# A macaron transformer on one core: the turned query by two transfers between partitions instead of a second product

## The chip, the cores and the metric

One core of a Trainium2 chip runs the whole program in one launch. The metric is the time of one execution on the device, in microseconds (us). The kernel before was timed in three runs: 1578.59, 1580.87 and 1582.71 us, so its median is 1580.87 us. The profile is of one further execution, which took 1578.82 us.

## What is computed

The input is x of 16 rows, each 512 tokens by 128 features, in float32. Six sublayers follow each other, each with a layer norm in front and a residual sum behind:

1. a small piecewise network per token ("kan" in the code), with half weight
2. causal attention with 16 query heads and 4 key and value heads of 8 features each, and a rotary embedding on queries and keys
3. the network of 1 again, with half weight
4. a mixture of 8 experts; each expert takes the 128 best tokens of each row; with half weight
5. a linear recurrence over the tokens, in pairs of rows
6. the mixture of 4 again, with half weight

The change lies in sublayer 2, in the rotary embedding of the queries. The reference writes it as

```python
def rotate_half(x):
    half = x.shape[-1] // 2
    x1, x2 = (x[..., :half], x[..., half:])
    return jnp.concatenate((-x2, x1), axis=-1)
...
q = (x @ Wq).reshape(bsz, seq_len, NH, HD).transpose(0, 2, 1, 3)
...
q = q * cos + rotate_half(q) * sin
k = k * cos + rotate_half(k) * sin
```

So of the 8 features of a head, the first four take the last four with a minus sign, and the last four take the first four, each times the sine of the token's angle.

## The kernel before

**Layout.** Inside the attention a row's queries lie with 128 partitions = 16 heads x 8 features (head by head) and the 512 tokens along the free axis. `attn_in` (L435) makes them. It normalises the row (`norm`, L296, with a turned copy of it through TensorE in `turned`, L333), multiplies it by `wq` into the PSUM tile `ps_pa` (L443), and VectorE multiplies that by the cosine table `rope[:, 0, :]` into `rope_a` (L444). The rotated query is a second product, of the same row by `wqr`, which is `wq` with the halves of each head exchanged (L572, L573), into `ps_pb` (L449). VectorE multiplies it by the sine table `rope[:, 1, :]`, which holds the sign, into `rope_b` (L450), and GpSimd adds the two (L465). Keys and values come from `ps_kv` (L457, L461).

**Splitting and packs.** The scores are made with bfloat16 products that together keep float32 accuracy: `parts` (L406) splits the sum into three bfloat16 parts, one step on ScalarE (L409) and three on GpSimd (L412, L415, L418), into `qpart`. `spread` (L421) stores the three parts to a scratch tensor `qs` in device memory (L425), `spread_keys` (L428) those of the keys to `ks`. From there the packs `qp` (four a row, in ten buffers) and `kp` (one a row, in three) are loaded (L508, L514), each as soon as its buffer's readers have been issued (the counter `taken`). All of these transfers are on SyncE's queue.

**Steps and turns.** The attention runs in steps, b = -1 to 15. In step b, `weights` (L699) makes the transposed scores of row b (L712), their exponentials on ScalarE (L715), and the causal mask on GpSimd (L717); `maxima` (L638) makes the scores of row b+1 (L652) and their row maxima on VectorE (L657, and L662 where several heads share a bank). `outputs` (L723) multiplies by the values (L738). Scores take their PSUM banks in turn from five (`next_bank`, L630), two a turn. A step has 44 turns: four packs by the eleven banks of `BANKS` (L624).

**Order within the engines.** The order on TensorE, VectorE, ScalarE and GpSimd is the order in which the Python program issues (`manual_schedule`, L222); SyncE's queue is ordered by the scheduler. All other work is written as generators: `stage_in` (kan of a row, then `attn_in`), `stage_out` (L770: the attention's output product through the tile `yT`, the second kan, then `gated`, L793, the normalisation (L320) and gate scores (L799) for the experts). Each generator goes on by one `yield` a turn. In the steady part (`paced`) each turn has a budget for every engine:

```python
MOST = {"pe": 1.5, "dve": 1.15, "act": 0.85, "pool": 1.45}
```

`need(...)` waits for a turn whose budget has that much left and takes it, `take(...)` takes without waiting, `bank(..., work)` waits for one of two PSUM tiles and for TensorE's budget. A reader of a PSUM tile is put in `later`, and issued at the begin of the next turn. Generators that stand earlier in the list are served first. `rope_b` and `yT` have the same tag and so share one buffer. At the end of a step `finish` runs turns of side work alone until the row after next is in.

The ramp is what comes before step 0 (`filling`): rows 0, 1 and 2 go through `attn_in` there; rows 3 to 15 go through it in steps 0 to 12. After step 15 come the experts and the recurrence.

Of the kernel before, what the change touches and what calls it, by code (L numbers as in the profile page):

```python
# [8 lines left out]
F32 = mybir.dt.float32  # L9
# [5 lines left out]
ALU = mybir.AluOpType  # L15
# [33 lines left out]
def tile_macaron(  # L49
# [55 lines left out]
    with ExitStack() as ph:  # L105
# [69 lines left out]
        kcst = cst.tile([P, D], F32, name="kcst")  # L175


        wq = cst.tile([D, NH, HD], F32, name="wq")
        nc.sync.dma_start(out=wq, in_=wq_in.rearrange("k (h d) -> k h d", d=HD))
        wk = cst.tile([D, 2, HD, NR], F32, name="wk")  # L180
        nc.sync.dma_start(out=wk[:, 0, :, :].rearrange("k d h -> k (d h)"), in_=wk_in)
        wv = cst.tile([D, KR], F32, name="wv")
        nc.sync.dma_start(out=wv, in_=wv_in)
        wo = cst.tile([D, D], F32, name="wo")
        rope = cst.tile([P, 2, S], F32, name="rope")
        nc.sync.dma_start(out=rope, in_=rope_in)
        out_weights()
        for b in range(1, B):
            load(b)
# [5 lines left out]
        wqr = cst.tile([D, NH, HD], F32, name="wqr")  # L195
# [41 lines left out]
        def need(**work):  # L237
            while paced[0] and any(w > room[e] for e, w in work.items()):
                yield
            for e, w in work.items():  # L240
                room[e] -= w

        def take(**work):

            for e, w in work.items():
                room[e] -= w
# [7 lines left out]
            for _ in range(turns if hurry[0] else 0):  # L254
                yield

        held, kan_held, hurry = [0], [0], [False]
# [75 lines left out]
        def turned(src, name, pool):  # L333
            ps = yield from bank([P, NT, P], F32, "ps_t", 0.55)
            for c in range(NT):
                nc.tensor.transpose(ps[:, c, :], src[:, c, :], ident)  # L336
            dst = pool.tile([P, S], F32, name=name)
            later.append(lambda: nc.scalar.copy(dst, ps.rearrange("p c q -> p (c q)")))
            yield
            take(act=0.6)  # L340
            freed()
            yield
            yield from rest(1)
            yield
            return dst
# [75 lines left out]
        def spread(part, heads, name):  # L421

            scr = tc.dram_tile([3, HD, heads, S], BF16, name=name)
            for i in range(3):
                nc.sync.dma_start(out=scr[i].rearrange("d h t -> h d t"), in_=part[:, i, :])  # L425
            return scr

        def spread_keys(part, name):  # L428
# [6 lines left out]
        def attn_in(b, st):  # L435
            _, xT = yield from norm(x[b])
            ka = w1p.tile([P, 2, P], F32, name="rope_ka")
            ta = w1p.tile([P, S], F32, name="rope_a")
            tb = w1p.tile([P, S], F32, name="rope_b", tag="yT")
# [3 lines left out]
            nc.tensor.matmul(pa, lhsT=wq.rearrange("k h d -> k (h d)"), rhs=xT, start=True, stop=True)  # L443
            later.append(lambda: nc.vector.tensor_mul(ta, pa, rope[:, 0, :]))  # L444
            yield
            take(dve=0.7)
            freed()
            pb = yield from bank([P, S], F32, "ps_pb", 0.9)
            nc.tensor.matmul(pb, lhsT=wqr.rearrange("k h d -> k (h d)"), rhs=xT, start=True, stop=True)  # L449
            later.append(lambda: nc.vector.tensor_mul(tb, pb, rope[:, 1, :]))  # L450
            yield
            take(dve=0.7)
            freed()
            pkv = yield from bank([P, 3, P], F32, "ps_kv", 1.3)
            for w in range(2):
                for j in range(NT):
                    nc.tensor.matmul(pkv[j * KR : (j + 1) * KR, w, :], lhsT=wk[:, w, :, :].rearrange("k d h -> k (d h)"),  # L457
                                     rhs=xT[:, bass.ts(j, P)], start=True, stop=True)
            pv = pkv[:, 2, :].rearrange("p (c n) -> p c n", n=KR)
            for c in range(NT):  # L460
                nc.tensor.matmul(pv[:, c, :], lhsT=xT[:, bass.ts(c, P)], rhs=wv, start=True, stop=True)  # L461
            later.append(lambda: nc.vector.tensor_mul(ka, pkv[:, 0:2, :], ropek))
            yield
            yield from need(pool=1.25)
            nc.gpsimd.tensor_tensor(ta, ta, tb, ALU.add)  # L465
            take(dve=0.4)

            va = VA[b % len(VA)]
            mine = [va[:, :, j::2, 2 * HD * j : 2 * HD * (j + 1)] for j in range(2)]
            if b < len(VA):  # L470
                nc.gpsimd.memset(va, 0.0)
                for to in mine:
                    nc.gpsimd.memset(to[:, :, :, HD : HD + 1], 1.0)

            def values():
                from_ = pv.rearrange("p c (r j d) -> p c r j d", j=2, d=HD)
                for j, to in enumerate(mine):
                    nc.vector.tensor_copy(to[:, :, :, 0:HD], from_[:, :, :, j, :])

            later.append(values)  # L480
            yield
            take(dve=0.4)
            freed()
            st["va"] = va
            if paced[0]:
# [18 lines left out]
            N = 3 * HD  # L504
            while taken[0] < NR * (b - NKP + 1):
# [35 lines left out]
        def prepare():  # L541
# [22 lines left out]
            freed()  # L564
            yield
            psc = yield from bank([P, 3, P], F32, "ps_kc3")
            centered(psc[:, 0, :], wq.rearrange("k h d -> k (h d)"))
# [4 lines left out]
            nc.vector.tensor_copy(wqr[:, :, 0:hh], wq[:, :, hh:HD])  # L572
            nc.vector.tensor_copy(wqr[:, :, hh:HD], wq[:, :, 0:hh])  # L573
# [196 lines left out]
        def stage_out(b, st):  # L770
            while len(st["out"]) < NR:
                yield
            if paced[0]:
                yield
                yield
            yT = yield from turned(st["y"].rearrange("p c r g d -> p c (r g d)"), "yT", w1p)
# [534 lines left out]
```

## Time and profile before

| what | value |
|---|---|
| median of three runs | 1580.87 us (1578.59 to 1582.71) |
| the profiled execution | 1578.82 us |
| its span, first to last instruction | 1577.0 us |
| mean granted TensorE clock | 0.985 |
| transfers on SyncE's and ScalarE's queues (q1) | 15.0% of 16 engines' span |
| L443 and L449, 32 records each (16 rows, two passes) | 0.593 us and 0.592 us a record |
| L444 and L450, 16 each | 0.678 us each |
| L465, 16 | 1.272 us each |
| L425, issue on SyncE's queue, 48 | 0.570 us each |

The profile names engines PE (TensorE matmul), PEld (its weight loads), DVE (VectorE), ACT (ScalarE), POOL (GpSimd) and SP (SyncE); a trailing q is an engine's queue. It gives for each engine the busy time, the share of the span, and the number of instructions; then the span in 40 equal slices, one digit each for the busy tenths, with 9 for 90% or more (a slice is 39.4 us). The chain of waits is the work that ended last, followed back from the last instruction to whatever released it; its rows have the start, the duration, the engine, the tile written and the line. The table of stretches gives for a part of the span its length, then the busy time and count of PE, PEld, DVE, ACT and POOL, then the granted clock, the share of the transfer engines, and GB/s. One product of the program in float32 appears as two records, of which the second begins before the first has ended.

### The profile page before, as it was taken

The page shows a single profiled execution, that of the slowest core. Times are in us where ns is not written, and L with a number is a line of the kernel's source. Part 1 is how long each engine was busy: PE and PEld are TensorE (multiplying, and loading weights), DVE is VectorE, ACT ScalarE, POOL GpSimd, SP SyncE. Part 2 cuts the span into 40 slices and gives each one's busy share as a digit, 9 for nine tenths or more (in the row PEclk, how much of TensorE's full clock was granted, in tenths as well). Part 3 has the DMA queues.
Part 4 walks back from the last instruction along what each step waited for, and adds up shares of the span by engine and source line. Part 5 has one row for each costly group of instructions (what it writes and reads, how often), then busy time and mean ns, then how long its engine had stood idle before and what let it go on. Part 6 is the DMA issues. An engine that isn't in the chain of part 4 may idle for free.

```text
span 1577.0 us, 33209 instructions
## 1 busy us (share of the span) xinstructions
PE 1480.0 (94%) x11889; PEld 1044.6 (66%) x11905; DVE 1085.1 (69%) x3574; ACT 960.5 (61%) x1852; POOL 923.8 (59%) x1439
## 2 busy tenths in 40 slices
PE   5679999999999999999999899999999999999997
PEld 2334454445445454444444489999998999999997
DVE  5587877878788788888888245865579665753333
ACT  3455767778788777777776865444454444544443
POOL 2535545556655564556454766667666666767773
PEclk8889999999999999999999999999999999999999
DMA  5220110122111210221031113222332233333332
GB/s 136 78 62 29 58 53 14 49 59 60 32 37 54 60 52 14 56 61 41 26 91 53 52 45 71 58 61 70 73 72 61 71 73 62 81 65 68 68 68 61
DMA packets 107467, 92.89 MB, mean 59 GB/s; under 512 B 23469, under 2 KB 95862, under 8 KB 107062
## 3 DMA queue, kind: packets, MB, share of 16 engines
q1 hardware_dynamic: 84464, 67.67, 15.0%
q0 software_dynamic: 21584, 22.89, 7.8%
q8 instruction: 94, 1.54, 0.4%
q14 instruction: 71, 0.58, 0.1%
q10 hardware_dynamic: 1254, 0.20, 0.1%
HBM read 59.20 MB, written 35.45 MB: 60 GB/s over the span
## 4 chain that ended last, share of the span: by engine, by line
PE 78%; DVE 11%; ACT 4%; issue 2%; POOL 1%; DMA 1%; SPq 1%; ACTq 0%; DVEq 0%; POOLq 0%
PE ps_h L1025 14%; PE ps_y L1038 14%; PE ps_av L738 9%; PE ps_st L712 7%; PE ps_sc L652 6%; PE acc L989 5%; DVE below L657 4%; PE ps_kg L385 4%; PE ps_s L356 3%; PE ps_t L336 3%; ACT pt L715 2%; PE ps_x L954 2%; PE ps_g L799 2%; ACT kan_h L375 1%; PE ps_ko L399 1%
## 5 line engine op out<-in xcount | busy, mean ns | idle before, releaser
L715 ACT ACTIVATE pt<-ps_st 128x512 f32<-128x512 f32 (+1 forms) x704 | 378.9, 567 | 127.2 <-PE ps_st L712 115.4
L717 POOL TENSOR_SCALAR_AFFINE_SELECT pt<-pt 128x128 f32<-128x128 f32 (+2 forms) x704 | 252.5, 367 | 315.2 <-ACT pt L715 309.1
L657 DVE CUSTOM_DVE_ANT_0 below<-ps_sc,causal 128x512 bf16<-128x512 f32 (+1 forms) x512 | 315.5, 616 | 102.1 <-PE ps_sc L652 86.2
L934 POOL DMA_INDIRECT xg<-xnd,tokI x256 | 253.0, 988 | 80.8 <-issue 36.4
L1027 ACT ACTIVATE mo<-ps_h 128x512 f32<-128x512 f32 x256 | 152.8, 597 | 217.3 <-PE ps_h L1025 215.2
L1025 PE MATMUL ps_h<-xin,mw 128*128 128x128 f32 x2048 | 272.5, 276 | 0.0
L1038 PE MATMUL ps_y<-mw,mo 128*128 128x128 f32 x2048 | 270.8, 275 | 0.0
L712 PE MATMUL ps_st<-qp,kp 128*128 128x512 bf16 (+3 forms) x1008 | 247.3, 301 | 24.7 <-DVE topped L657 18.6
L652 PE MATMUL ps_sc<-kp,qp 96*128 96x512 bf16 (+3 forms) x1024 | 255.0, 303 | 10.5 <-ACT pt L715 6.6
L1025 PEld LDWEIGHTS ps_h<-xin,mw 128*128 128x128 f32 x2048 | 250.3, 192 | 12.4 <-issue 9.9
L1038 PEld LDWEIGHTS ps_y<-mw,mo 128*128 128x128 f32 x2048 | 249.4, 192 | 1.0 <-DVE ye L1035 0.8
L712 PEld LDWEIGHTS <-kp 128*128 128x128 bf16 x1024 | 94.9, 100 | 191.3 <-issue 171.5
L375 ACT ACTIVATE kan_h<-kan_s,rbias,kw 128x512 f32<-128x512 f32 x256 | 207.5, 820 | 0.0
L1055 POOL DMA_INDIRECT sum<-mo,tokI x93 | 151.5, 1629 | 72.2 <-issue 15.9
L738 PE MATMUL ps_av<-pt,va 128*32 128x512 f32 (+3 forms) x2048 | 165.4, 440 | 1.4 <-POOL pt L717 1.2
L662 DVE TENSOR_REDUCE topped<-ps_sc 128x2 f32<-128x512 f32 (+1 forms) x192 | 127.0, 682 | 23.2 <-PE ps_sc L652 22.6
L652 PEld LDWEIGHTS <-qp 96*128 96x128 bf16 x1024 | 95.5, 98 | 67.2 <-issue 40.7
L738 PEld LDWEIGHTS ps_av<-pt,va 128*32 128x32 f32 x2048 | 53.4, 109 | 87.7 <-issue 44.2
L310 POOL TENSOR_TENSOR ln_rstd<-ln_rstd,mhalf 128x4 f32<-128x4 f32 x96 | 102.3, 1066 | 8.0
L309 POOL TENSOR_SCALAR ln_rstd<-ln_mv 128x4 f32<-128x4 f32 x96 | 22.1, 230 | 135.4 <-DVE ln_mv L307 134.5
L1044 DVE SCALAR_TENSOR_TENSOR ye<-ps_y,gainT,ye 128x128 fp32r<-128x128 f32 x83 | 29.0, 349 | 84.2 <-ACT ye L1041 84.0
L1044 DVE SCALAR_TENSOR_TENSOR parts<-ps_y,gainT,parts 128x128 fp32r<-128x128 f32 x80 | 27.9, 349 | 83.9 <-ACT parts L1041 83.8
(202 smaller groups left out, 2279.4 us busy)
## 6 DMA issues: line engine op xcount, KB each, us to landing
qp<-qs SPq DMA_DIRECT2D x64, 288.0 KB
xnd<-kan_x SPq DMA_DIRECT2D x32, 256.0 KB
sum<-x SPq DMA_DIRECT2D x62, 128.0 KB
qs<-qpart SPq DMA_DIRECT2D x48, 128.0 KB
kp<-ks SPq DMA_DIRECT2D x48, 96.0 KB
x<-in_L_attn_x_dram SPq DMA_DIRECT2D x16, 256.0 KB
mw<-in_L_ffn_w_dram SPq DMA_DIRECT2D x16, 256.0 KB
xg<-xnd,tokI POOLq DMA_INDIRECT x256, 2.5
```

Source lines behind the costliest of these rows:

```text
L375: nc.scalar.activation(h, sk[half], AF.Relu, bias=rbias[:, half, v : v + 1], scale=kw1[:, half, v : v + 1])
L652: nc.tensor.matmul(v[:, u, 0:n], lhsT=qp[r][0:MXR, g, bass.ts(c, P)], rhs=kp[0:MXR, r, 0:n], start=alone, stop=(u == len(gs) - 1), skip_gr ...
L657: nc.vector.tensor_tensor_reduce(below[:, 0:n], v[:, 0, 0:n], causal[:, S - n : S], 1.0, LOWEST, ALU.add, ALU.max, accum_out=maxs[:, h, c ...
L712: nc.tensor.matmul(v[:, u, 0:n], lhsT=kp[ROWS, r, bass.ts(c, P)], rhs=qp[r][ROWS, g, c * P : S], start=True, stop=True)
L715: nc.scalar.activation(o, v[:, :, 0:n], AF.Exp, scale=HD ** -0.5)
L717: nc.gpsimd.affine_select(out=dg, in_=dg, compare_op=ALU.is_ge, fill=0.0, base=0, pattern=[[0, len(gs)], [1, P]], channel_multiplier=-1)
L738: nc.tensor.matmul(po[32 * g : 32 * g + 32, c * P : S], lhsT=va[:, c, r, :], rhs=pt[:, g, OFF[c] : OFF[c] + n], start=(c == 0 and not odd) ...
L934: nc.gpsimd.indirect_dma_start(out=xgs[i // E % 2][:, i % E, :], out_offset=None, in_=xnd[b], in_offset=bass.IndirectOffsetOnAxis(ap=tokI[ ...
L1025: nc.tensor.matmul(pst[:, f, :], lhsT=mw1[e][:, bass.ts(f, P)], rhs=xins[i // E % 2][:, i % E, :], start=True, stop=True)
L1027: nc.scalar.activation(hs[u], pst, AF.Gelu)
L1038: nc.tensor.matmul(py, lhsT=hs[u][:, f, :], rhs=mw2[e][:, f, :], start=(f == 0), stop=(f == NF - 1))
L1055: nc.gpsimd.indirect_dma_start(out=sums[k, b], out_offset=bass.IndirectOffsetOnAxis(ap=tokI[g][:, n : n + 1], axis=0), in_=added[b % 2 * ( ...
```

## The change

For the rows of the ramp (`direct`) little is different: the rotated query is still a second product, and as the sine table is stored differently, GpSimd subtracts instead of adding. For all later rows the second product is gone. VectorE multiplies `ps_pa` twice, first by the sine table into a float32 view of `qpart`, then by the cosine table into `rope_a`. Two transfers of 64 partitions by 512 float32 values carry the first result to the other half of the partitions, into `rope_b`, and GpSimd adds four turns later than it did. For this the partitions are ordered feature by feature (`(d h)` instead of `(h d)`), so that the two halves of all heads lie in the two halves of the partitions; `wq`, `wqr`, the table and the stores to `qs` follow that order, and the table is loaded in four transfers. A flag, `y_held`, keeps `rope_b` and `yT` from holding their buffer at once. In the steady part, three turns lie between the stores to `qs` and `ks` and the loads of the packs.

```diff
-        wq = cst.tile([D, NH, HD], F32, name="wq")
-        nc.sync.dma_start(out=wq, in_=wq_in.rearrange("k (h d) -> k h d", d=HD))
+        wq = cst.tile([D, HD, NH], F32, name="wq")
+        nc.sync.dma_start(out=wq.rearrange("k d h -> k (d h)"), in_=wq_in)
...
-        nc.sync.dma_start(out=rope, in_=rope_in)
+        halves = [slice(a * P // 2, (a + 1) * P // 2) for a in range(2)]
+        for a in range(2):
+            for w in range(2):
+                rows = a ^ w
+                src = rope_in[rows * HD // 2 : (rows + 1) * HD // 2, w, :]
+                nc.sync.dma_start(out=rope[halves[a], w, :], in_=src.unsqueeze(1).to_broadcast([HD // 2, NH, S]))
...
-                nc.sync.dma_start(out=scr[i].rearrange("d h t -> h d t"), in_=part[:, i, :])
+                nc.sync.dma_start(out=scr[i].rearrange("d h t -> (d h) t"), in_=part[:, i, :])
...
-            later.append(lambda: nc.vector.tensor_mul(ta, pa, rope[:, 0, :]))
-            yield
-            take(dve=0.7)
-            freed()
-            pb = yield from bank([P, S], F32, "ps_pb", 0.9)
-            nc.tensor.matmul(pb, lhsT=wqr.rearrange("k h d -> k (h d)"), rhs=xT, start=True, stop=True)
-            later.append(lambda: nc.vector.tensor_mul(tb, pb, rope[:, 1, :]))
-            yield
-            take(dve=0.7)
-            freed()
+            direct = filling[0]
+            if direct:
...
+            else:
+                while y_held[0]:
+                    yield
+                y_held[0] = True
+                unturned = qpart.rearrange("p i t -> p (i t)")[:, 0 : 2 * S].bitcast(F32)
+                later.append(lambda: nc.vector.tensor_mul(unturned, pa, rope[:, 1, :]))
+                yield
+                take(dve=0.7)
+                yield from need(dve=0.7)
+                nc.vector.tensor_mul(ta, pa, rope[:, 0, :])
+                freed()
+                tb = w1p.tile([P, S], F32, name="rope_b", tag="yT")
+                for a in range(2):
+                    nc.sync.dma_start(out=tb[halves[a], :], in_=unturned[halves[1 - a], :])
...
-            yield from need(pool=1.25)
-            nc.gpsimd.tensor_tensor(ta, ta, tb, ALU.add)
+            if direct:
+                yield from need(pool=1.25)
+                nc.gpsimd.tensor_tensor(ta, ta, tb, ALU.subtract)
+                y_held[0] = False
             take(dve=0.4)
...
             st["va"] = va
+            if not direct:
+                for _ in range(4):
+                    yield
+                yield from need(pool=1.25)
+                nc.gpsimd.tensor_tensor(ta, ta, tb, ALU.add)
+                y_held[0] = False
+                yield
             if paced[0]:
                 yield
             qp_steps = parts(ta, qpart, nc.scalar.copy, 1.15, act=0.6)
...
             qs = spread(qpart, NH, f"qs{b}")
             N = 3 * HD
+            for _ in range(3 if paced[0] else 0):
+                yield
             while taken[0] < NR * (b - NKP + 1):
                 yield
...
+            while y_held[0]:
+                yield
+            y_held[0] = True
             yT = yield from turned(st["y"].rearrange("p c r g d -> p c (r g d)"), "yT", w1p)
             po = yield from bank([P, NT, D], F32, "ps_o", 0.9)
             for c in range(NT):
                 nc.tensor.matmul(po[:, c, :], lhsT=yT[:, bass.ts(c, P)], rhs=wo, start=True, stop=True)
+            y_held[0] = False
```

More of the change, by code (lines that the diff above doesn't have):

```diff
@@ L194, in tile_macaron @@
         hh = HD // 2
-        wqr = cst.tile([D, NH, HD], F32, name="wqr")
+        wqr = cst.tile([D, HD, NH], F32, name="wqr")
         identb = cst.tile([P, P], BF16, name="identb")
@@ L255, in rest @@
                 yield
-        held, kan_held, hurry = [0], [0], [False]
+        held, kan_held, hurry, y_held = [0], [0], [False], [False]
         def bank(shape, dtype, name, work=0.0):
@@ L438, in attn_in @@
             ta = w1p.tile([P, S], F32, name="rope_a")
-            tb = w1p.tile([P, S], F32, name="rope_b", tag="yT")
             qpart = w1p.tile([P, 3, S], BF16, name="qpart")
@@ L442, in attn_in @@
             pa = yield from bank([P, S], F32, "ps_pa", 0.9)
-            nc.tensor.matmul(pa, lhsT=wq.rearrange("k h d -> k (h d)"), rhs=xT, start=True, stop=True)
-            later.append(lambda: nc.vector.tensor_mul(ta, pa, rope[:, 0, :]))
-            yield
-            take(dve=0.7)
-            freed()
-            pb = yield from bank([P, S], F32, "ps_pb", 0.9)
-            nc.tensor.matmul(pb, lhsT=wqr.rearrange("k h d -> k (h d)"), rhs=xT, start=True, stop=True)
-            later.append(lambda: nc.vector.tensor_mul(tb, pb, rope[:, 1, :]))
-            yield
-            take(dve=0.7)
-            freed()
+            nc.tensor.matmul(pa, lhsT=wq.rearrange("k d h -> k (d h)"), rhs=xT, start=True, stop=True)
+            direct = filling[0]
+            if direct:
+                later.append(lambda: nc.vector.tensor_mul(ta, pa, rope[:, 0, :]))
+                yield
[4 more added lines that the diff above has]
+                y_held[0] = True
+                pb = yield from bank([P, S], F32, "ps_pb", 0.9)
+                nc.tensor.matmul(pb, lhsT=wqr.rearrange("k d h -> k (d h)"), rhs=xT, start=True, stop=True)
+                tb = w1p.tile([P, S], F32, name="rope_b", tag="yT")
+                later.append(lambda: nc.vector.tensor_mul(tb, pb, rope[:, 1, :]))
+                yield
+                take(dve=0.7)
+                freed()
+            else:
[5 more added lines that the diff above has]
+                yield
+                take(dve=0.7)
+                yield from need(dve=0.7)
+                nc.vector.tensor_mul(ta, pa, rope[:, 0, :])
+                freed()
+                tb = w1p.tile([P, S], F32, name="rope_b", tag="yT")
+                for a in range(2):
+                    nc.sync.dma_start(out=tb[halves[a], :], in_=unturned[halves[1 - a], :])
             pkv = yield from bank([P, 3, P], F32, "ps_kv", 1.3)
@@ L484, in attn_in @@
             st["va"] = va
+            if not direct:
[4 more added lines that the diff above has]
+                y_held[0] = False
+                yield
             if paced[0]:
@@ L504, in attn_in @@
             N = 3 * HD
+            for _ in range(3 if paced[0] else 0):
+                yield
             while taken[0] < NR * (b - NKP + 1):
@@ L566, in prepare @@
             psc = yield from bank([P, 3, P], F32, "ps_kc3")
-            centered(psc[:, 0, :], wq.rearrange("k h d -> k (h d)"))
+            centered(psc[:, 0, :], wq.rearrange("k d h -> k (d h)"), wq)
             centered(psc[:, 1, :], wk[:, 0, :, :].rearrange("k d h -> k (d h)"), wk[:, 0, :, :])
@@ L571, in prepare @@
             yield
-            nc.vector.tensor_copy(wqr[:, :, 0:hh], wq[:, :, hh:HD])
-            nc.vector.tensor_copy(wqr[:, :, hh:HD], wq[:, :, 0:hh])
+            nc.vector.tensor_copy(wqr[:, 0:hh, :], wq[:, hh:HD, :])
+            nc.vector.tensor_copy(wqr[:, hh:HD, :], wq[:, 0:hh, :])
             nc.vector.tensor_copy(wk[:, 1, 0:hh, :], wk[:, 0, hh:HD, :])
@@ L775, in stage_out @@
                 yield
+            while y_held[0]:
+                yield
+            y_held[0] = True
             yT = yield from turned(st["y"].rearrange("p c r g d -> p c (r g d)"), "yT", w1p)
```

## The prediction

> **What bounds the kernel now.** I began with the page's busy times, then its slices, the chain of work that ended last, and the table of stretches.
>
> ```profile
> PE 1480.0 (94%) x11889; PEld 1044.6 (66%) x11905; DVE 1085.1 (69%) x3574; ACT 960.5 (61%) x1852; POOL 923.8 (59%) x1439
> ...
> PE   5679999999999999999999899999999999999997
> ...
> DVE  5587877878788788888888245865579665753333
> ...
> PE 78%; DVE 11%; ACT 4%; issue 2%; POOL 1%; DMA 1%; SPq 1%; ACTq 0%; DVEq 0%; POOLq 0%
> ```
>
> PE is busy nearly throughout, but in slices 4 to 21 (some 120 to 870 us), where the attention runs and the change lies, DVE is busy for eight tenths too. So a PE saving may or may not reach the end. The chain says where it does. From it, around one of the second products of the rotation:
>
> ```profile
> 410.82 0.22 PE ps_st L712
> 411.04 0.22 PE ps_sc L652
> 411.26 0.86 PE ps_pb L449 x2
> 412.12 0.22 PE ps_st L712
> ```
>
> Here PE is the path, and L449 takes 0.86 us of it. It is so at each of the 13 products that the change removes: 0.86 us ten times, 0.91 three times. Twenty us later the chain of the same step reads
>
> ```profile
> 432.69 0.27 PE ps_st L712
> 432.95 0.18 PE ps_sc L652
> 433.13 0.02 issue
> 433.16 0.56 DVE below L657
> 433.71 0.01 DVE topped L657
> 433.72 0.06 DVE kan_x L320
> 433.78 0.12 issue
> 433.90 0.34 DVE kan_x L320
> 434.24 0.47 DVE below L657
> ```
>
> and goes on like that to 438.0: DVE is the path, and PE waits for a score bank. With five banks and two taken a turn, scores of turn k need DVE to be through with turn k-3. Such stretches come twice a step. Timed by the first exponential of each row, the steps of rows 5 to 8 last 48.7, 53.8, 48.7, 53.8 us, light and heavy in turn, since L443/L449 fall at a step's edge: a heavy step holds two pairs, a light one none. The table of stretches for one of each (PE, PEld, DVE, ACT, POOL):
>
> ```profile
> 411.40:465.20 53.80, 51.84 (x423) 26.88 (x424) 42.33 (x139) 40.53 (x76) 29.87 (x64) 1.00 0.15 45
> 465.20:513.90 48.70, 46.99 (x373) 24.33 (x373) 39.93 (x136) 40.04 (x75) 29.19 (x61) 1.00 0.17 49
> ```
>
> In the heavy one the chain has 42.3 us of PE, 7.0 of DVE, 4.0 of ACT.
>
> **The change, part by part.**
>
> *The removed product.* The built order has 13 L449 products fewer (rows 3 to 15) and otherwise the same matmuls. 10 x 0.86 + 3 x 0.91 = 11.3 us of PE, all on the path before. DVE still makes two multiplications a row, 0.68 us each (L444, L450), both now from `ps_pa`. POOL's addition, 1.27 us, stays. The Trainium skill (Perfetto Trace Analysis, "Identifying the Most-Contended Engine") holds matmul busy time a poor measure and wants the share of the weight loads: in the heavy step above 50%, beside 96% of matmul. It speaks against reading PE as full; cut to the PE share of that step's chain, 42.3 of 53.8, the gain would be an estimated 8.9 us in place of 11.3.
>
> *What moves.* This is the term I find largest. The number of turns is the same, 817 to the end of the attention, so nothing is gained by fewer turns; only by shorter ones. The addition is put four turns later, so the splitting (three POOL steps that ask 1.15 to 1.3 of a turn's 1.45) falls in turns 11 to 18 of a step instead of 6 to 13. There the normalisation for the gate of another row asks POOL for 1.4, and it is behind in the list. So its four L320 go to turns 21 and 22 (before: 16 and 17 in a heavy step, 13 and 14 in a light one), and its transposes and gate product behind turn 25.
>
> I priced the instructions of each turn by their spacing in the trace: PE 0.22, 0.16, 0.11 for scores of 512, 384, 256 columns, 0.86 a 512-wide float product, 0.99 and 1.43 the two parts of L738, 0.44 four transposes; DVE 0.62 and 0.49 for L657, 0.62 for L662, 0.22 a bn_stats, 0.33 an L320, 0.61 a 128x512 multiplication; ACT 0.50 to 0.52 an exponential or copy, 0.72 a relu. PE, DVE and ACT in us:
>
> - turns 16 to 24: heavy 6.4, 9.0, 8.7; light 6.8, 7.7, 8.5; changed 5.2, 9.2, 8.9
> - turns 38 to 43: heavy 4.9, 5.8, 5.7; light 3.2, 5.8, 5.7; changed 3.2, 5.8, 5.7
> - PE in the other turns: heavy 36.9; light 34.7; changed 37.2
>
> If a stretch lasts as long as its fullest engine, and PE sets the rest, a heavy step is 36.9 + 9.0 + 5.8 = 51.7 (it lasted 53.8), a light one 34.7 + 8.5 + 5.8 = 49.0 (48.7), a changed one 37.2 + 9.2 + 5.8 = 52.2. The mean of heavy and light is 50.3. PE has 0.87 less to do, but 1.4 of what it did inside DVE's stretch is now done outside it. So steps 5 to 8 lose 4 x 1.9 = 7.6 us in place of gaining.
>
> The same sum for the others, changed less before: steps 0 to 4 -1.6, -1.9, -0.1, -4.6, -1.1 (there side work is moved between steps too); step 9 +2.8; steps 10 to 15 -0.2, +0.8, +0.8, +0.8, 0, 0. All: -9.3 + 10.4 + 2.2 = **+3.3 us**. The 11.3 is in it.
>
> *Two transfers, 128 KB each,* on SP's queue, then POOL's addition waits for them. No row shows a copy between partitions. Bounds: L693 waits for the landing of L691 1.5 us in the mean, 3.9 at most; a 288 KB load of `qp` took 4.29 on the chain. With an issue of 0.57 (L425) the second lands 2 to 5 us after DVE's product. The addition is eight turns behind it, 8 x 51.2/44 = 9.3 us. Cost: 0, covered by the turns. Without that cover POOL would stand still with L717's masks behind it, L738 behind those: up to 13 us for each us of lateness, over 13 rows. By the Trainium skill (SBUF — State Buffer, "The DMA setup-cost knee") such a copy takes 2 + 0.3 us, an estimate below the wait of 3.9; the sum is the same. In SP's order the two stand behind the row maxima of half 0, issued some twenty turns earlier, and ahead of those of half 1, which wait for DVE anyway: 0.
>
> *Loads three turns behind the stores.* In a steady step they go from turn 13 to 21 (the addition's five and these three); the fourth `qp` stays at turn 22, held by the pack's readers. The first reader comes at turn 44. Twenty-three turns, 27 us, cover a store and a load of 4.3 each: 0. SP idles less in front of a landing (L508 waited 14.3 us in all), which nobody was waiting for: no gain.
>
> *yT and rope_b share a buffer.* The held flag delays no turn: yT begins in the same turns. ACT's copy into it now follows POOL's addition by three turns (3.5 us) instead of seven; the addition takes 1.27 and one mask. Taken 0; bounds 0 and 13 x 0.6 = 8 us, if ACT stands for one exponential each time.
>
> *Start.* The rope table comes in four transfers instead of one, and the two `kb` go ahead of x1's load, so x1 is issued some 3 us later than 10.0. DVE clears packs until 26.4 and reads x1 then: 0. PE's L557 at 18.9 needs `kb` and `wout`: 0 to +1. The other layout of wq and of the stores moves the same bytes by as many rows: within 0.3 either way.
>
> **Sum.** 1578.8 (the profiled execution; its span 1577.0) + 3.3 = 1582.1. The median of the runs, 1580.9, is 2.1 above that execution, so the median after is **1584**.
>
> **Rivals.**
>
> *The saving comes through.* PE runs up to three turns ahead of DVE, so a stretch need not last as long as DVE. For it: every L449 is on the chain, and at 420.95 and 433.1 DVE begins its stretch on PE's word, without arrears. Against it: the light and heavy steps differ by 5.1 us where PE's load differs by 3.5. 1580.9 - 11.3 = 1569.6.
>
> *Slower: every step is a heavy one.* Heavy steps last 2.1 us over my sum, light ones 0.3 under it. Changed steps are like the heavy in turns 0 to 24. If they have the heavy surplus, steps 5 to 9 last 4 x 54.3 + 55.6 = 272.8 us, against 255.9 measured before: +16.9, less 7.1 in the rest: +9.8, so 1591. It decides from a surplus of about 1 us a changed step.
>
> *POOL waits for the transfers* past nine us: one us of lateness gives some 1597.
>
> That the change doesn't do what it says is excluded by the order: the product is gone in 13 rows and stays in 3.
>
> **Chances.** Forecast 0.42, saving through 0.26, heavy steps 0.26, POOL waits 0.06. About 0.3% (4.7 us) is what a measurement of this kernel can tell from no change. The forecast's 1584 lies near that edge: of its 0.42 I give 0.29 to within, 0.12 to slower, 0.01 to faster. The saving gives 0.24 to faster, 0.02 to within; heavy steps 0.24 to slower, 0.02 to within; POOL 0.05 and 0.01. Faster 0.25, within 0.34, slower 0.41. The range takes in the saving and the heavy steps: 1569 to 1596. The forecast's own is 1579 to 1589.
>
> **What would show it.** Steps of rows 5 to 8 all alike, at 52 to 53 us; on the chain, DVE and ACT longer in turns 16 to 25, with L320 at its end; PE's busy time down by some 15 us (26 records of 0.59). No wait of POOL on `rope_b`'s transfers, none of ACT's yT copy on POOL. I am wrong if steps 5 to 8 stay under 51 us (PE's lead covers DVE), or if a DMA is named as what ended POOL's idle time.

## The result and the profile after

The changed kernel takes 1590.28 us (median of seven runs, 1588.84 to 1598.25), the kernel before 1581.52 us beside it (seven runs, 1578.59 to 1582.71). The ratio is 1.0072 [1.0059, 1.0086], some 11.4 us of 1581: slower. Ratios here and below are those on record; the quotient of the two medians is 1.0055 here, and over all runs it lies within 0.0017 of the ratio. The forecast was 1584 and the range, which took in two rivals, 1569 to 1596; the forecast's own range was 1579 to 1589.

The profiled execution has a span of 1590.9 us, 13.9 above that of before. The page gives first the busy times, further down the chain's shares:

```profile
PE 1474.2 (93%) x11879; PEld 1039.7 (65%) x11879; DVE 1095.2 (69%) x3574; ACT 959.8 (60%) x1852; POOL 919.2 (58%) x1439
...
DVE  5588888787878778888888345765669665753333
...
PE 75%; DVE 15%; ACT 3%; issue 3%; POOL 1%; DMA 1%; ACTq 0%; DVEq 0%; POOLq 0%
```

DVE has exactly as many instructions as before (3574) and is busy 10.1 us longer; its share of the chain went from 11 to 15%. So some instructions of DVE became longer, and more of the path runs through DVE.

Where the time is, by the first exponential of each row (us):

| part | before | forecast for it | after |
|---|---|---|---|
| steps 0 to 4 | 254.1 | -9.3 | 242.6 (-11.5) |
| steps 5 to 9 | 255.9 | +10.4 | 272.4 (+16.5) |
| steps 10 to 15 | 295.2 | +2.2 | 302.4 (+7.2) |
| ramp; what follows step 15 | 108.5; 663.3 | 0 | 109.5; 664.0 |

Steps 5 to 8 last 53.5, 53.7, 55.3, 53.7 us. Two of them in the table of stretches (length, then PE, PEld, DVE, ACT, POOL, the clock, transfers):

```profile
405.50:459.30 53.80, 49.43 (x398) 25.31 (x397) 42.74 (x137) 40.53 (x77) 29.35 (x64) 1.00 0.17 50
459.30:514.60 55.30, 50.92 (x398) 25.72 (x397) 42.84 (x137) 40.39 (x77) 29.26 (x63) 0.97 0.16 48
```

PE has 0.9 to 2.4 us less than in a heavy step before and the step is as long or longer: PE now stands. The longer of the two holds 3.4 us at half the clock (0.51), right behind that step's wait at L707, which is shown further down (the table of stretches again):

```profile
488.40:491.80 3.40, 3.40 (x15) 1.27 (x15) 3.37 (x9) 1.81 (x4) 2.48 (x6) 0.51 0.60 192
```

PE's 398 records take 1.5 us more in that step. In 120 to 870 us there are three such stretches, 10.2 us in all; before it was 10.2 us too, in 207.4 to 214.2 and 282.4 to 285.9. So the clock does not make the difference of the two kernels, but it bears on the parts in the table: before, all of it lay in steps 2 and 3.

The waits of PE in 100 to 840 us name two places. First before (total, times, longest), where the keys' product (L457) had no wait of this kind in these 740 us:

```profile
PE ps_m L672 <- DVE topped L662: 1.5, 2, 1.2
```

and after, where L672 has become L707 and L457 has become L481:

```profile
PE ps_m L707 <- DVE topped L697: 10.1, 10, 1.2
...
PE ps_kv L481 <- DVE rope_a L473: 8.0, 9, 1.2
```

L707 transposes the row maxima; it follows DVE's stretch in the middle of a step. L481 makes the keys; it waits for the second multiplication of the query, which holds the PSUM tile. The chain of one step into L707:

```profile
484.55 0.09 DVE topped L697
484.64 0.43 issue
485.07 0.37 DVE ln_mv L312 x4
485.44 0.18 DVE topped L697
485.62 0.31 issue
485.93 1.56 DVE kan_x L325 x2
487.49 0.61 DVE topped L697
488.10 0.04 issue
488.15 0.33 PE ps_m L707
```

Two L325 take 1.56 us. The prediction priced one (L320 before) at 0.33. The timeline of the same place, with GpSimd:

```profile
485.78 1.27 POOL L384 TENSOR_TENSOR x<-x,kcst 128x512 f32<-128x512 f32 x1
485.93 1.56 DVE L325 TENSOR_SCALAR kan_x<-x,ln_mv,ln_rstd 128x128 f32<-128x128 f32 x2
...
488.01 0.59 DVE L325 TENSOR_SCALAR kan_x<-x,ln_mv,ln_rstd 128x128 f32<-128x128 f32 x2
```

L384 is GpSimd's addition of a constant to the residual of another row. The pair of L325 that begins inside it takes 1.56, the pair 2.1 us later 0.59. The groups of the whole attention show it too. Before (count, busy us, mean ns):

```profile
L324 DVE TENSOR_TENSOR kan_x<-x,ln_rstd 128x512 f32<-128x512 f32 x38 | 31.1, 818 | 0.0
...
L320 DVE TENSOR_SCALAR kan_x<-x,ln_mv,ln_rstd 128x128 f32<-128x128 f32 x52 | 17.1, 370 | 0.0
```

and after, where the same lines are L329 and L325:

```profile
L329 DVE TENSOR_TENSOR kan_x<-x,ln_rstd 128x512 f32<-128x512 f32 x37 | 33.5, 904 | 0.0
L325 DVE TENSOR_SCALAR kan_x<-x,ln_mv,ln_rstd 128x128 f32<-128x128 f32 x52 | 23.4, 490 | 0.0
```

Over all of 100 to 860 us, ten L325 are longer than 0.50 us and 17 L329 longer than 0.90; before it was one and nine. Not all of them lie beside L384 itself: nine of the ten L325 do, and eight of the 17 L329. The other nine L329 and one L325 lie beside masks, which stand behind L384 in GpSimd's queue:

```profile
488.71 1.95 POOL L752 TENSOR_SCALAR_AFFINE_SELECT pt<-pt 128x256 f32<-128x256 f32 x4
...
489.13 1.13 DVE L329 TENSOR_TENSOR kan_x<-x,ln_rstd 128x512 f32<-128x512 f32 x1
```

### The profile page after: what moved, and what is told of

It reads as the page before. It is cut to its first block, busy times and chain, and to the rows that moved or that the text cites. A ratio compares the mean times of both kernels' runs of the same rounds, so it can differ in the third digit from the quotient of the medians.

```text
span 1590.9 us, 33274 instructions
## 1 busy us (share of the span) xinstructions
PE 1474.2 (93%) x11879; PEld 1039.7 (65%) x11879; DVE 1095.2 (69%) x3574; ACT 959.8 (60%) x1852; POOL 919.2 (58%) x1439
## 4 chain that ended last, share of the span: by engine, by line
PE 75%; DVE 15%; ACT 3%; issue 3%; POOL 1%; DMA 1%; ACTq 0%; DVEq 0%; POOLq 0%
PE ps_h L1064 14%; PE ps_y L1077 13%; PE ps_av L773 9%; PE ps_st L747 7%; PE ps_sc L687 6%; PE acc L1028 5%; DVE below L692 5%; PE ps_kg L390 4%; PE ps_s L361 4%; PE ps_t L341 3%; DVE topped L697 2%; DVE ln_st L308 2%; PE ps_x L993 2%; PE ps_ko L404 2%; ACT pt L750 2%
## 5 line engine op out<-in xcount | busy, mean ns | idle before, releaser
L752 POOL TENSOR_SCALAR_AFFINE_SELECT pt<-pt 128x128 f32<-128x128 f32 (+2 forms) x704 | 251.4, 366 | 337.5 <-ACT pt L750 334.2
L747 PE MATMUL ps_st<-qp,kp 128*128 128x512 bf16 (+3 forms) x1024 | 253.8, 302 | 25.1 <-DVE topped L692 18.8
L697 DVE TENSOR_REDUCE topped<-ps_sc 128x2 f32<-128x512 f32 (+1 forms) x192 | 127.3, 683 | 21.6 <-PE ps_sc L687 21.2
L773 PEld LDWEIGHTS ps_av<-pt,va 128*32 128x32 f32 x2048 | 53.6, 110 | 86.6 <-issue 51.6
```

The source lines that it names most:

```text
L697: nc.vector.tensor_reduce(maxs[:, h : h + len(gs), c], v[:, :, 0:n], AX.X, ALU.max)
L747: nc.tensor.matmul(v[:, u, 0:n], lhsT=kp[ROWS, r, bass.ts(c, P)], rhs=qp[r][ROWS, g, c * P : S], start=True, stop=True)
L752: nc.gpsimd.affine_select(out=dg, in_=dg, compare_op=ALU.is_ge, fill=0.0, base=0, pattern=[[0, len(gs)], [1, P]], channel_multiplier=-1)
L773: nc.tensor.matmul(po[32 * g : 32 * g + 32, c * P : S], lhsT=va[:, c, r, :], rhs=pt[:, g, OFF[c] : OFF[c] + n], start=(c == 0 and not odd) ...
```

## The experiments

Every ratio is to the kernel before, timed on the same chip. Three chips were used. On that of the first four runs the part behind step 15 took some 701 us instead of 663, in all four kernels, and on that of the last four some 673 to 677, so only ratios and steps are compared across chips.

The theory that stood at first was the prediction's: the moved work ("order"). Its first rival: the PSUM tile that is held longer ("bank"). A third, the collision of L325 and L329 with L384 and the masks behind it ("collision"), came out of the profile above.

**The addition without its four turns.**

```diff
             if not direct:
-                for _ in range(4):
-                    yield
                 yield from need(pool=1.25)
                 nc.gpsimd.tensor_tensor(ta, ta, tb, ALU.add)
```

> The changed kernel with the four turns in front of POOL's addition taken out, so the splitting starts four turns sooner and POOL waits for the transfers if they are not there. Theory 'order' (the splitting, moved to turns 11 to 18 of a step, pushes the gate's normalisation into the stretch that DVE sets): steps 5 to 9 fall from 53.5-56.2 us to about 50-53 and the total to 1578-1584. Rival 'bank' (PE waits for the bank of ps_pa, held until the second multiplication): unchanged, 1588-1592, with the same waits of ps_kv on L473. Rival 'transfers' (the copies between partitions are what costs): slower than the changed kernel, 1595 or more, POOL's addition named as waiting for a DMA, some 2 us in each of 13 rows.

Ratio 1.0000 [0.9982, 1.0017]: the loss is gone, the gain is not there. GpSimd waits for the transfers once, for 0.5 us. But the edit moves all side work, so it can't say by what the loss goes: PE's wait at L481 falls from 8.0 to 1.4 us, and with it go three of the ten long L325 and seven of the 17 long L329.

**Both multiplications in one turn.**

```diff
                 later.append(lambda: nc.vector.tensor_mul(unturned, pa, rope[:, 1, :]))
+                later.append(lambda: nc.vector.tensor_mul(ta, pa, rope[:, 0, :]))
                 yield
-                take(dve=0.7)
-                yield from need(dve=0.7)
-                nc.vector.tensor_mul(ta, pa, rope[:, 0, :])
+                take(dve=1.4)
                 freed()
```

> The changed kernel with both multiplications of ps_pa issued in one turn, so that its bank is free a turn sooner; the addition stays late. 'Bank': PE's waits of ps_kv on L473 (9.9 us in ten rows) go, total 1578-1583. 'Order': the splitting moves a turn at most, total 1586-1592. 'Transfers': no change.

Ratio 0.9960 [0.9939, 0.9982], faster than before; steps 5 to 8 are 52.0 us each, and of the wait at L481 0.4 us are left. The order moves here too (the keys come a turn sooner, and five L325 are long instead of ten), so this alone separates nothing either.

**The move alone.** The second product is back for every row; the late addition, the late loads and the flag stay.

```diff
-                later.append(lambda: nc.vector.tensor_mul(unturned, pa, rope[:, 1, :]))
+                later.append(lambda: nc.vector.tensor_mul(ta, pa, rope[:, 0, :]))
...
-                for a in range(2):
-                    nc.sync.dma_start(out=tb[halves[a], :], in_=unturned[halves[1 - a], :])
+                pb = yield from bank([P, S], F32, "ps_pb", 0.9)
+                nc.tensor.matmul(pb, lhsT=wqr.rearrange("k d h -> k (d h)"), rhs=xT, start=True, stop=True)
+                later.append(lambda: nc.vector.tensor_mul(tb, pb, rope[:, 1, :]))
```

> The changed kernel with the second product put back for all rows in place of the two transfers; the late addition, the loads three turns behind and the held flag stay. So against the kernel before it is the move alone, against the changed kernel the product alone. If the saving came through and the move cost some 20 us ('order' in its plain form): 1599-1603. If the product now stands in turns that DVE sets anyway, and taking it out gained nothing ('buried'): 1588-1594, steps 5 to 9 at 53-56 us as in the changed kernel. 'Transfers': about 1581, as before.

Ratio 1.0084 [1.0058, 1.0111]. So the move alone costs 13 us, before anything is saved. Its waits have L707 on L697 at 10.1 us, as the changed kernel, and no wait at L481; ten L325 and 17 L329 are long. At the time this looked as if the product's removal were worth only 0.0012. That reading was wrong, since the changed kernel pays for the held tile besides, as the fifth run shows.

**The product made cheap, nothing moved.** The kernel before, with the second product of rows 3 to 15 replaced by a bfloat16 product of a unit matrix into the same tile (left out: the rotated query of these rows). The order of all instructions stays.

```diff
-            nc.tensor.matmul(pb, lhsT=wqr.rearrange("k h d -> k (h d)"), rhs=xT, start=True, stop=True)
+            if filling[0]:
+                nc.tensor.matmul(pb, lhsT=wqr.rearrange("k h d -> k (h d)"), rhs=xT, start=True, stop=True)
+            else:
+                nc.tensor.matmul(pb.rearrange("p (c q) -> p c q", c=NT), lhsT=identb,
+                                 rhs=identb.unsqueeze(1).to_broadcast([P, NT, P]), start=True, stop=True)
```

> The kernel before, in its own order, with the second product of rows 3 to 15 replaced by a bfloat16 product of the unit matrix into the same bank (so the rotated query is left out there): some 0.22 us of PE in place of 0.86, 8.3 us less over 13 rows, with no instruction moved. If what L449 takes on the chain is worth its time when nothing moves: 1572-1575. 'Buried' (DVE sets those turns as soon as PE is shorter): 1578-1581.

Ratio 0.9952 [0.9936, 0.9968], 7.6 us less (5.1 to 10.1) of the 8.3 expected. The product was on the path, as the chain had said.

**The second multiplication two turns up.** The two multiplications in one turn again, but the budgets are asked for where they were. So exactly 13 instructions change their turn, and nothing else.

```diff
                 later.append(lambda: nc.vector.tensor_mul(unturned, pa, rope[:, 1, :]))
+                later.append(lambda: nc.vector.tensor_mul(ta, pa, rope[:, 0, :]))
                 yield
                 take(dve=0.7)
                 yield from need(dve=0.7)
-                nc.vector.tensor_mul(ta, pa, rope[:, 0, :])
                 freed()
```

> The changed kernel, with one thing other: the second multiplication is issued right behind the first, two turns earlier; every other instruction keeps its turn, and the budgets are asked for as before. 'Bank' (TensorE stands at L481 because ps_pa's PSUM tile is held until the second multiplication, and this is most of the loss): the waits of ps_kv on rope_a, 8.0 us of PE and 12.4 us of its weight loads in nine steps, go; 9 to 13 us come back, ratio to before 0.999 to 1.002, a step of rows 5 to 8 about 52.5 us where the changed kernel has 54. 'Order' (the work that moved out of VectorE's stretch is the loss, the bank wait only lies where TensorE would have stood anyway): the wait goes to another line, ratio 1.005 to 1.009, steps 53.5 to 55.

Ratio 1.0030 [1.0015, 1.0044], beside 1.0072 of the changed kernel on this chip: 6.6 us come back. The waits of PE:

```profile
PE ps_st L747 <- DVE topped L692: 17.9, 40, 0.8
PE ps_m L707 <- DVE topped L697: 10.1, 10, 1.2
PE ps_sc L687 <- ACT pt L750: 8.3, 18, 0.7
```

L481 is gone, and L707 stands untouched at 10.1; steps 5 to 8 last 54.2, 54.4, 52.9, 52.9 us, the first two with 3.4 us each at half the clock. The tile is one cost by itself, smaller than 'bank' wanted (9 to 13), larger than 'order' allowed. Against the move alone (1.0084), which has no wait at L481 either and the same 10.1 at L707, the ratio is 0.0054 lower: some 8.5 us, which is what the product's removal is worth in the moved order. The two ratios are from two chips, and by their intervals the 8.5 is uncertain by some 5 us.

**Without the constant.** L384 is left out (the constant of the first and third sublayer's residual); its place and budget stay, and nothing else moves.

```diff
-                    nc.gpsimd.tensor_tensor(x[b], x[b], kcst.unsqueeze(1).to_broadcast([P, NT, D]), ALU.add)
+                    pass
```

> The changed kernel without GpSimd's addition of the constant in L384 (left out: the constant of the first and third sublayer's residual); its place and budget stay, so that no other instruction moves. 'Collision' (L325 takes 0.47 us in the mean where it took 0.37 because L384 now runs beside it, and it stands at the end of VectorE's stretch): L325 back to 0.34 to 0.38 us, VectorE's busy time 5 to 8 us lower, 4 to 8 us of the time come back, ratio to before 1.002 to 1.005. 'Only busy' (it is longer, but the stretch is set by the row maxima and L697 behind it): L325 shorter, ratio within 0.002 of the changed kernel's. 'Other partner' (the splitting or the masks slow it): L325 stays at 0.45 or above and the ratio stays too.

Ratio 0.9990 [0.9980, 0.9999]: 13 us come back, more than 'collision' expected. L325 falls to 0.347 us in the mean, none is long, and steps 5 to 8 last 52.4 us each. The long L329 beside masks are gone too. But 1.27 us of GpSimd's work a time are left out as well.

**Both in one turn and the addition at once**, the edits of the first two runs together.

> Both multiplications asked for and issued in one turn, and the addition without the four turns: the two undone parts together. Alone they gave ratios to before of 1.000 (addition at once) and 0.996 (both in one turn), where the changed kernel had 1.007. If the bank and the place of the addition are two costs that add: 0.988 to 0.992, 12 to 19 us under before, with the 11.3 us of the product then saved in full. If they are one cost, seen twice: 0.995 to 1.000. If GpSimd now stands for the transfers (the addition comes four turns sooner, about four behind the second multiplication): a wait of rope_a on a DMA on GpSimd, and 1.000 or more.

Ratio 0.9970 [0.9959, 0.9981], in the band of one cost seen twice; but the two edits move other work too, so this does not decide it. Steps 5 to 8 are 51.2, 49.8, 49.8, 49.8 us. GpSimd's waits in 100 to 860 us now name the transfers among the longest (total, times, longest):

```profile
POOL rope_a L512 <- DMA rope_b<-qpart: 2.7, 5, 1.4
```

Five waits of 2.7 us in all. Eight L325 and 16 L329 are long here: seven and seven beside L384, five L329 beside the addition of the rotation (L512), the rest beside masks and the splitting. So the collision has more than one partner.

**The changed kernel again**, as a control for the three runs above.

> The changed kernel itself, on the chip of these runs, so that the other three are compared with it directly. Every theory: ratio to before 1.005 to 1.010 (1.0072 in its own comparison), steps of rows 5 to 8 of 53 to 55 us, waits of ps_kv on rope_a of 8 us on PE in nine steps.

Ratio 1.0072 [1.0059, 1.0085], steps 5 to 8 at 55.1, 53.7, 55.3, 53.7 us.

**The kernel before without the constant**, the edit of the sixth run (the same part is left out).

> The kernel before without GpSimd's addition of the constant (left out: the constant of the first and third sublayer's residual), all else in its turn. Without it the changed kernel had a ratio of 0.999 where it has 1.0072 with it, 13 us less. Before, one L320 and nine L324 are stretched (over 0.50 and 0.90 us), 3.9 us above the means of 0.347 and 0.745 us that stand without the constant; in the changed kernel ten and 17, 13.4 us. 'The move brought the collision': 0 to 4 us less, ratio 0.997 to 1.000, so that 9 to 13 us of the 13 belong to the change. 'The constant costs the same in both' (it is GpSimd's 1.27 us, or the row's next reader that waits for it): 0.990 to 0.993.

Ratio 0.9986 [0.9975, 0.9997]: 2.2 us, where the same edit gave the changed kernel 13. So some 10.5 us of the collision are what the move brought.

**The constant later.** The changed kernel, whole, with L384 five turns on in the first network of a step; its budget stays where it was, and nothing else moves.

```diff
-                if t == 1:
+                if t == 6:
                     nc.gpsimd.tensor_tensor(x[b], x[b], kcst.unsqueeze(1).to_broadcast([P, NT, D]), ALU.add)
```

> The changed kernel, whole, with L384 issued behind the seventh relu instead of the second (turn 24 of a step instead of 19, turn 2 of the next instead of 36); its budget is asked for where it was and nothing else moves. 'Collision': L325 and L329 back to about 0.35 and 0.75 us, VectorE's busy time 8 to 13 us lower, ratio 0.998 to 1.002, steps of rows 5 to 8 of 52.4 us as without the constant. 'GpSimd's load' (its queue is shorter without L384, and the masks behind it come sooner): L325 short, but the ratio stays at 1.004 to 1.008.

Ratio 0.9992 [0.9982, 1.0003], steps 5 to 8 at 52.4, 52.7, 52.4, 52.4 us: all that leaving it out had given, with GpSimd's work still there. DVE's timeline in the place shown above, now

```profile
484.44 0.59 DVE L325 TENSOR_SCALAR kan_x<-x,ln_mv,ln_rstd 128x128 f32<-128x128 f32 x2
484.95 0.69 DVE L697 TENSOR_REDUCE topped<-ps_sc 128x4 f32<-128x512 f32 x1
485.55 0.59 DVE L325 TENSOR_SCALAR kan_x<-x,ln_mv,ln_rstd 128x128 f32<-128x128 f32 x2
...
486.67 0.88 DVE L329 TENSOR_TENSOR kan_x<-x,ln_rstd 128x512 f32<-128x512 f32 x1
```

with L384 at 487.93, behind all of them. The waits of PE:

```profile
PE ps_kv L481 <- DVE rope_a L473: 7.8, 9, 1.2
...
PE ps_m L707 <- DVE topped L697: 3.5, 10, 0.5
```

This is the mirror of the fifth run: L707 fell from 10.1 to 3.5, L481 is all but untouched. 'GpSimd's load' falls as it was put, since the ratio did not stay. What the edit does not separate is L384 itself from the masks that it held up: the four masks shown above now begin at 485.99, and L329 beside them takes 0.88. Nor does it separate the clock: 3.4 us at half the clock are left in 120 to 870 us, where the changed kernel had 10.2; at half speed 6.8 us are worth at most 3.4 (an estimate). In the changed kernel each of the three stretches stands behind a wait at L707.

**Both repaired**, the edits of the fifth and the tenth run.

> The last edit and the second multiplication two turns up, together; the moved work stays where the change put it. Alone the one gave back 6.6 us (1.003), the constant's absence 13 us (0.999). If the two are separate costs: 0.993 to 0.997, 5 to 11 us under before, steps of rows 5 to 8 at 50.5 to 51.5 us, and then nothing of the loss is left for the place of PE's work. If they are one cost in part (the same VectorE stretch, met at two ends): 0.997 to 1.001, steps about 52 us.

Ratio 0.9952 [0.9938, 0.9965]. The two costs add: 1.0072 less 0.0042 less 0.0080 is 0.9950. Steps 5 to 8 last 51.6, 51.8, 51.5, 51.5 us, just above the band expected for separate costs.

```profile
404.40:456.20 51.80, 49.46 (x399) 25.34 (x397) 41.11 (x138) 40.04 (x76) 28.93 (x62) 1.00 0.18 51
```

The work is the changed kernel's, instruction for instruction, but DVE (third) is at 41 us instead of 42.8.

**The fastest.** The seventh run, with L384 behind the fifth relu (`if t == 4`).

> Both multiplications in one turn, the addition without its four turns (0.997 as it was), and L384 behind the fifth relu: the candidate for the fastest. There eight L325 and 16 L329 were stretched, 11.8 us above the means without the constant. If VectorE's stretch is the path there too: about half of it to all of it comes back, ratio 0.989 to 0.993. If TensorE sets the steps there (49.8 us for rows 5 to 8): 0.995 to 0.998.

Ratio 0.9924 [0.9909, 0.9938], 1579.94 us beside 1592.18: faster than before by some 12 us, and than the changed kernel by some 23. Steps 5 to 8 are 50.8, 49.3, 49.3, 49.3 us. PE is busy for 48.2 of one of them:

```profile
458.20:507.50 49.30, 48.22 (x398) 25.12 (x397) 41.33 (x138) 39.93 (x77) 29.11 (x63) 1.00 0.19 54
```

One L325 and nine L329 are still long here, four of the nine beside the addition L512 and only two beside L384.

## Why the prediction was right and wrong

The sum of the case, each step from a pair of runs (1581 us to one):

| from, to | ratio | us |
|---|---|---|
| before, its own collisions taken out | 1.0000 to 0.9986 | -2.2 |
| the move without collisions (worked out: 1.0084 - 0.0080) | to 1.0004 | +2.8 |
| the product removed (1.0084 against 1.0030) | to 0.9950 | -8.5 |
| the tile held until the second multiplication | to 0.9992 | +6.6 |
| the collision of L325 and L329 with L384 | to 1.0072 | +12.7 |

The second line is no run: it takes for the move alone the collision's price in the changed kernel, since both have the same ten and 17 long instructions. Its 2.8 us lie inside the intervals of the runs it comes from. The product's line compares two runs on two chips, which also differ in the sine multiplication's place and the two transfers. The first and the last two lines are shown by edits that move or leave out one instruction of the program's text. The clock is in every line and is not separated: in 120 to 870 us the move alone has 10.2 us at half the clock, as before, and the kernel with both repaired none.

- **The product, -11.3, all on the path.** The sign and the place hold: 7.6 of 8.3 with a cheap product in its place, 8.5 in the moved order. The prediction's other figure, 8.9, came from PE's share of the chain; the intervals of these runs hold both it and 11.3 and do not decide between them.
- **The move is the largest term.** Right: it alone costs 13 us. The gate normalisation does go to turns 21 and 22. But most of the price was put on the wrong thing. The prediction had PE's work leave DVE's stretch: 1.9 us a step, with 0.87 of product saved in it, so 2.8. With both repaired and the work still in its new place, steps 5 to 8 take 206.4 us, where they took 205.0 before, with no stretch at half the clock in either; four products less, that leaves some 1.2 us a step (worked out from one execution each). Over the whole program 2.8 us are left, and most of what the move costs is that L325 and L329 now fall on L384 and the masks behind it.
- **Luck.** The sum was +3.3, and 1590 lies in the wide range because errors ran against each other. With the two repaired costs out, the same change came to -7.6 (-9.8 to -5.5), some 11 us under the sum (2.2 of them are the collisions of the kernel before); the two costs that the sum did not hold, 6.6 and 12.7, added 19. The sum priced the move at 3.3 + 11.3 = 14.6 us and the run of the move alone gave 13.3, nearly the same for largely another reason.
- **The step that failed** is "0.33 an L320" in the list of prices, with "DVE 0.61 a 128x512 multiplication" beside it: durations from the old order were carried to a new one, where the instruction has another neighbour. The mean became 0.49. The profile of before had it: in 109 to 860 us L320 has a minimum, median and maximum of 331, 342 and 1203 ns there, L324 675, 686 and 1330. The prediction used neither maximum. With the collision gone the steps are at 52.4, beside the 52.2 of the sum, though that sum held no wait at L481; with both repaired they are 0.6 under it.
- **The tile.** "DVE still makes two multiplications a row, both now from `ps_pa`" counted their duration and not that the tile is held for two turns longer, with L481 queued on PE behind it and the scores behind L481. That was 6.6 us and stood nowhere, neither in the sum nor among the bounds.
- **The slower rival** gave 1591 and 272.8 us for steps 5 to 9; 1590 and 272.4 came. Its reason is not the one: it carried the heavy steps' surplus of 2.1 us over, and heavy steps keep 53.7 us without the constant. A number that fits is no proof of its cause.
- **Transfers, 0.** Right. The bytes of one row move from 461.4 to 462.9 us, the multiplication ends at 460.15: 2.8 us, inside 2 to 5. In the changed kernel GpSimd never waits for them; it does where the addition comes at once: 0.5 us in the first run, 2.7 in the seventh, 2.8 in the last.
- **yT and the start.** ACT's copy into yT never waits for GpSimd; the ramp is 1.0 us longer, the upper end given, but in two other executions it is 110.1 (control) and 110.0 (before without the constant), so the 1.0 is not clear of noise. The loads three turns later and the other layouts were not tried by themselves.
- **What would show it.** All steps alike: yes, but at 53.5 to 55.3. DVE longer on the chain with L320 at the end of its stretch: yes, the row is there, and it was thought to be there for another reason. PE's busy time went down by 5.8 us, not 15: the page has only ten matmul records fewer where 26 are gone, as some were missing before. In two executions where none is missing (before without the constant, the constant later) it is 9.3 less. The 15 also counted the two records of a product one after the other (26 x 0.59), though they overlap: by the prediction's own 0.86 and 0.91 it is 11.3.

## What to carry to other kernels

When a change moves an instruction, price it at its new neighbours: look at the spread of its durations (minimum, median, maximum) and see what runs on the other engine in the long ones. Count not only how long a reader of a PSUM tile takes but until when the tile is held and what stands behind it in the queue. To test one cost of a schedule that shifts with every edit, move the one instruction and leave its budget where it was: then nothing else moves, and two such edits here added up to within 0.0002.

## What the hardware showed

In the control run nine L325 begin inside an L384, and all end at the same place, whenever they began: those that began 0.15, 0.48 and 0.55 us into an L384 of 1.27 us took 1.20, 0.87 and 0.80, so that each ends 1.35 us after L384's start. Alone it takes 0.34. So L325 is held for the whole rest, not slowed. L329, with two inputs, ends some 0.55 us behind L384, as if most of its 0.68 were still to do: it began at 0.49, 0.70 and 0.92 and took 1.34, 1.12 and 0.89, so that each ends 1.8 us after L384's start. The other way round, in the seventh run, an L384 that began 0.1 us behind an L329 took 1.71. Beside four masks in a row (L752, 1.95 us) an L329 took 1.13. Not all of VectorE's instructions are held: the statistics (L303 before, L308 in the control run) keep 0.28 us beside the constant, in 16 cases before and seven in the control run, and the one multiplication from PSUM that fell beside it before, an L444, took 0.69, as another did alone.

The Trainium skill (SBUF — State Buffer, "Who interferes with whom") has this rule: a VectorE `tensor_scalar` in one of its two-port modes, or a VectorE instruction with two inputs in SBUF, shares a port pair with GpSimd's reads; whichever comes first keeps it for the whole instruction, and the other stands still. The runs agree, with the numbers above; which mode L325 runs in they do not show. The rule bears on this change, which gave VectorE's instructions new neighbours on GpSimd, and the prediction did not weigh it.
